# Five small moves in a two-layer decoder kernel: one output product dealt later in its turn, two copies shared between engines, two sets of tiles in other PSUM banks, and an earlier limit for the experts' statistics

## The chip, the cores and the metric

The kernel runs on one core of one Trainium2 chip. The metric is the device time in microseconds of one execution, lower is better. A core has a matrix engine (TensorE, PE in the profile; its weight loads are listed apart as PEld), a vector engine (VectorE, DVE), a scalar engine (ScalarE, ACT), GpSimd (POOL) and SyncE (SP), which here issues most of the DMAs. Each engine works through a queue of its own in order, and engines wait for one another by semaphores. TensorE writes its results to PSUM, eight banks of 128 partitions by 512 fp32 numbers, from which VectorE or ScalarE copy ("empty") them.

## The reference, cut to what matters

Two decoder layers over x (8 x 112 x 512), with a context of 8 x 375 x 128. All is fp32.

```python
x = x + attn0(layernorm(x))          # 32 heads of 64, 8 kv heads, rope, window 64, sinks
x = x + xattn0(layernorm(x), ctx)    # 16 heads; keys of the 375 context rows by low rank maps
x = x + ffn0(layernorm(x))           # ternary weights, gelu
x = x + attn1(layernorm(x))          # 16 heads of 128, 4 kv heads, rope, causal mask
x = x + xattn1(layernorm(x), ctx)    # 16 heads of 32, causal mask
x = x + ffn1(layernorm(x))           # two rounds of gated experts
```

In attention 0 and cross attention 0 a head's result is multiplied by its rows of an output matrix Wo and added to x. In cross attention 0, `ctx_lat = ctx_c @ w_kc_kv` and then `ctx_lat @ Wo.T`; both matrices are weights, so the kernel multiplies them with each other first ("folds" them) and uses the product.

## The kernel before, in words

**Tiles.** The 896 rows of x (8 batches of 112) stand in SBUF as 7 tiles of 128 rows, numbered 0 to 6. Transposed activations (xT) are in two halves of four batches, 448 columns each. A tile of x may straddle two batches, so it is complete for an output product only when certain batches are done (`completed`: after the first half of a turn pair tile 0 at once and tiles 1, 2 later; after the second half tiles 3, 4 at once and 5, 6 later).

**PSUM.** One pool with two buffers for each of three tags: `mm` (one bank, helper `mm`), `s` (two banks, helper `wide`, the score banks) and `t` (one bank, helper `turning`, for transposes). The third request for a tag waits until the first buffer has been emptied.

**Order of work.** TensorE's order is the order in which the program is written (its manual schedule). The other engines' orders are laid out by a planner, which simulates the program with costs of its own: of the instructions ready at a time it takes the one written first. `with tc.issue_after(i)` puts an instruction behind instruction i in the queue of its engine, if they are on the same one. `weave(main, filler)` (L237) deals filler steps between main steps: each step has a cost, and after a main step filler is taken as long as the cost of the filler done, plus half of the next one's, is at most the filler's total times the share of main done. The rest comes at the end.

**The attention pipeline (L410 to L457).** Attention 0 has 8 turns: 4 groups of 8 heads by 2 halves of the batches. Each turn has 4 units (a batch each). A unit's main steps are two transposes of the normalised probabilities p (ppt, L404, emptied to pT at L405), the scores two units ahead (ps, L608), and the contexts (po, L625, emptied to oT at L630). Softmax of a unit (L374 to L394): VectorE adds the mask (L382) and takes the maximum (L385), ScalarE does eight exponentials (L388), VectorE takes the reciprocals (L391), GpSimd scales (L393). A turn is two weaves: units 0 and 1, filled with the preparation of the next turn and then the late output products of the turn before; units 2 and 3, filled with the early output product of this turn. The lines are

```python
filler, late = ready or (prepare(n + 1) if n < end else []), outputs(n - 1, True) if n else []
ready, early = None, []
...
weave(mains(n, range(units - ahead)), filler + late)
...
weave(mains(n, range(units - ahead, units)), outputs(n, False) + early + extra(n))
```

Preparing a turn is one key and four query products (pr_k, pr_q: L235 called from L543), each followed by the rope: ScalarE copies with a bias (raw, L547), SP issues four DMAs that turn halves of the rows (L552), VectorE multiplies (L555), GpSimd multiplies and adds (L554, L556) into kT or qT. An output product (po_at, L361 and L365) is 4 matmuls with wo in two parts, and VectorE's addition to x (L366). Turn 7, the last, is woven in the next stage's `finale` (L878 for cross attention 0), with context transposes (pkv, L875), layernorm steps and the first fold.

**Cross attention 0.** A fold for each of 4 groups of 4 heads (`fold_steps`, L688 to L721): pB, four pV (L716, emptied to vo at L717) and two pR (L708, emptied to wr at L712), all in `mm` banks; the order is pB, pV, pV, pR, pR, pV, pV. Folds 1 to 3 are filler of the turns before their group (at about 433, 534 and 635 us). A turn's preparation: two query products pq_x (L235, emptied at L779) and eight key products pk_x (L783, emptied to kr at L784), a batch and half a group each. Odd batches use a `turning` bank, even ones an `mm` bank. Turn 0's keys stand in a list written by hand in `after` (L895), among transposes of x (pt_xa, L310).

**Cross attention 1, `go` (L1213).** There are sixteen units of softmax over 8 heads; the first five are woven together, with this filler: values pev (L1170, emptied to ev at L1171, odd batches of the second half by ScalarE, others by VectorE), the transposes of tiles 4, 5 and 6 (pt_xa, L310, in `mm` banks, emptied to xT by ScalarE at L314) and four query products peq. The later ones are woven one by one, with half an output product each (po_e, L361 and L365).

**The experts.** `ffn_1` begins with the layernorm of all 7 tiles into res (L1311; statistics L285, L286, root L274, scaling L289), each behind `copied[0]`, the last copy of transposed probabilities (L405). Then TensorE transposes res (pt_ff, L310) and does the first expert's products (pf).

Of the kernel before, what the change touches and what calls it, by code (L numbers as in the profile page):

```python
# [155 lines left out]
def decoder(ctx: ExitStack, tc: tile.TileContext, i: dict, out: bass.AP):  # L156
    nc = tc.nc
# [30 lines left out]
    x = cpool.tile([P, NT, D], F32, name="x")  # L188
# [4 lines left out]
    spans, n = _spans(_COLS)  # L193
# [7 lines left out]
    rspans, n = _spans(_ROWS)  # L201
# [14 lines left out]
    eps5 = cpool.tile([P, 1], F32, name="eps5")  # L216
# [9 lines left out]
    def wide(name):  # L226

        return psum.tile([P, 2, D], F32, tag="s", name=name)
# [8 lines left out]
    def weave(main, filler):  # L237


        whole, extra = sum(m[0] for m in main), sum(f[0] for f in filler)  # L240
        at, k, done, parted = 0.0, 0, 0.0, True

        def fill():
            nonlocal k, done, parted
            done += filler[k][0]
            filler[k][1]()
            k += 1
            parted = True

        for cost, step, *gap in main:  # L250
            if gap and not parted and k < len(filler):
                fill()
            step()
            parted = False
            at += cost
            while k < len(filler) and done + filler[k][0] / 2 <= extra * at / whole:
                fill()
        while k < len(filler):
            fill()

    def run(steps):
        for _, step, *_ in steps:
            step()
# [71 lines left out]
    def entering(pool, xT, name, tiles, bufs, bank=None):  # L335

        xn = {}

        def norm():
            xn.update(zip(tiles, normed(pool, tiles, name, bufs)))  # L340

        return [(0.0, norm)] + [(0.45, lambda k=k: turned_tile(xn[k], xT, k, name, bank)) for k in tiles]

    spread, copied = [], []


# [63 lines left out]
    def pipeline(turns, units, ahead, prepare, scores, contexts, outputs, extra, begun=None, finale=None, between=False, keys_early=()):  # L410

        queue = [(n, u) for n in range(len(turns)) for u in range(units)]

        def scored(k):
            return [(1.2, lambda: scores(*queue[k]))] if k < len(queue) else []

        def mains(n, us):
            steps = []
            for u in us:
                coming, own = scored(n * units + u + ahead), contexts(n, u)
                if between:
                    steps += own[:2] + coming + own[2:]
                else:
                    steps += coming + own
            return steps

        if begun is None:
            run(prepare(0) + extra(-1))
            for k in range(ahead):
                run(scored(k))
        for k in range(begun or (ahead if begun is None else 0), ahead):
            run(scored(k))
        end = len(turns) - 1
        ready = None
        for n in range(end + (finale is None)):
            filler, late = ready or (prepare(n + 1) if n < end else []), outputs(n - 1, True) if n else []  # L440
            ready, early = None, []
            if begun is None and n == 0:
                run(filler[:3])
                filler = filler[3:]
            weave(mains(n, range(units - ahead)), filler + late)
            if n in keys_early:
                early, *ready = prepare(n + 2)
                early = [early]
            weave(mains(n, range(units - ahead, units)), outputs(n, False) + early + extra(n))
        if finale is None:  # L450
            run(outputs(end, True))
        else:
            fillers, after = finale(outputs(end - 1, True) + outputs(end, False) + outputs(end, True))
            for u, filler in enumerate(fillers):
                weave(mains(end, [u]), filler)
            after()
# [231 lines left out]
    def fold_steps(pool, g, loads, kept):  # L688

        wq, woT, kk, ranks = loads  # L690
        rk = pool.tile([P, 4, 64], F32, tag="rk", bufs=1, name=f"rk_{g}")
        wr = pool.tile([P, NC, 256], F32, tag="wr", name=f"wr_{g}")
        vo = wpool.tile([P, 4, D], F32, tag="w", name=f"vo_{g}")
        kept.update(wr=wr, krw=ranks[:, 12:, :].rearrange("p a b -> p (a b)"), vo=vo)

        def rank():
            ps = mm(f"pB_{g}")
            for h in range(4):
                accumulate(
                    ps[:, h * 64 : (h + 1) * 64], [(kk[:, 3 * h + c, :], ranks[:, 3 * h + c, :]) for c in range(3)]  # L700
                )
            nc.vector.tensor_copy(rk.rearrange("p a b -> p (a b)"), ps[:, :256])

        def queries(c):
            ps = mm(f"pR_{g}_{c}")
            for k in range(2):
                for h in range(4):
                    nc.tensor.matmul(  # L708
                        ps[:, k * 256 + h * 64 : k * 256 + (h + 1) * 64],
                        wq[:, h, (c + k) * P : (c + k + 1) * P], rk[:, h, :], start=True, stop=True,  # L710
                    )
            nc.scalar.copy(wr[:, c : c + 2, :].rearrange("p a b -> p (a b)"), ps)  # L712

        def values(h):
            ps = mm(f"pV_{g}_{h}")
            nc.tensor.matmul(ps, kk[:, 12 + h, :], woT[:, h, :], start=True, stop=True)  # L716
            nc.vector.tensor_copy(vo[:, h, :], ps)  # L717

        v = [(0.9, lambda h=h: values(h)) for h in range(4)]
        q = [(1.7, lambda c=c: queries(c)) for c in (0, 2)]  # L720
        return [(2.5, rank), v[0], v[1], *q, v[2], v[3]]  # L721
# [27 lines left out]
    def cross_attention_0():  # L749
# [16 lines left out]
        def prepare(n):  # L766

            g, hf = turns[n]
            f, nm, qpool = folds[g], name(n), pool if hf else epool
            held[n].update(  # L770
                qr=[qpool.tile([P, HT], F32, tag="qr", name=f"qr_{nm}_{j}") for j in range(2)],
                kr=[qpool.tile([P, HB, L], F32, tag="kr", name=f"kr_{nm}_{j}") for j in range(2)],
            )

            def queries(j):
                ps = mm(f"pq_{nm}_{j}")
                at = slice(j * P, (j + 1) * P)
                accumulate(ps[:, :HT], [(f["wr"][:, c, at], xT[hf][:, c, :]) for c in range(NC)])
                nc.scalar.copy(held[n]["qr"][j], ps[:, :HT])  # L779

            def keys(j, b):
                ps = (turning if b % 2 else mm)(f"pk_{nm}_{j}_{b}")
                nc.tensor.matmul(ps[:, :L], f["krw"][:, j * P : (j + 1) * P], kvT[:, b, :], start=True, stop=True)  # L783
                nc.scalar.copy(held[n]["kr"][j][:, b % HB, :], ps[:, :L])  # L784

            steps = []
            for j in range(2):
                steps.append((3.0, lambda j=j: queries(j)))
                steps += [(0.65, lambda j=j, b=b: keys(j, b)) for b in batches(n)]
            return steps  # L790
# [354 lines left out]
    def cross_attention_1(npool, tpool):  # L1145
# [66 lines left out]

        def go():  # L1213
            values, queries, *outs = more
            enter = entering(npool, xT, "xa1", [4, 5, 6], 3, mm)
            fill = outs + enter[:1] + values[:2] + enter[1:2] + values[2:3] + enter[2:3] + values[3:]
            fill += enter[3:] + queries
            outs, units = outputs(), [divmod(k, 2 * HB) for k in range(4 * HB)]

            def steps(k):  # L1220
                *turn, add = contexts(*units[k])
                if k + 3 < len(units):
                    return turn + [(1.0, lambda: scores(*units[k + 3]), True), add[:2]]
                return turn + [add]

            scores(*units[2])
            weave([m for k in range(5) for m in steps(k)], fill)

            for k in range(5, len(units)):
                weave(steps(k), (outs[9:12] if k == len(units) - 1 else outs[k - 6 : k - 5]) if k > 5 else [])  # L1230
            run(outs[12:])
            pool.release()

# [52 lines left out]
    def ffn_1():  # L1286
        with (
# [3 lines left out]
            res = rpool.tile([P, NT, D], F32, tag="res", bufs=1, name="res")  # L1291
# [16 lines left out]
            w4 = rpool.tile([P, NT, P], F32, tag="w4", bufs=1, name="w4")  # L1308
            nc.gpsimd.memset(w4, 0.0)
            for tiles in GROUPS:  # L1310
                layernorm([x[:, k, :] for k in tiles], [res[:, k, :] for k in tiles], eps5, f"ff1_{tiles[0]}", copied[0])  # L1311
            for k in range(NT):
                with tc.issue_after(spread[0]):
                    nc.gpsimd.tensor_tensor(x[:, k, :], x[:, k, :], res[:, k, :], ALU.add)
# [115 lines left out]
            with tc.manual_schedule(engines={mybir.EngineType.PE}):  # L1430
                tail = []
                for j in range(2):
                    src, dst, base = (res, nxt, res) if j == 0 else (nxt, x, x)
                    xT, kept = new_halves(f"ff1_{j}"), {}
# [64 lines left out]
```

## Time and profile before

| | |
|---|---|
| median of 3 runs | 1862.39 us (1861.94 to 1867.62) |
| profiled execution, its own time | 1863.88 us |
| its span in the profile | 1862.0 us, 19727 instructions |
| mean granted TensorE clock | 0.996 |
| DMA | 108.68 MB, mean 58 GB/s |
| fp32 copy of 128x512 from PSUM | 0.69 us on VectorE (vo), 0.59 us on ScalarE (wr) |
| eight exponentials of a softmax | 3.0 us |

The profile's page gives, for one execution, each engine's busy time, the chain of work that ended last, and groups of instructions with their mean duration and the idle time before them. A line names the engine, the line of the kernel (it can be that of a helper: L235 is any accumulated product, L310 any transpose of activations), the output and its inputs. A wait "PE a <- ACT b" is time in which TensorE stood still before writing a, and the last thing it needed was ScalarE's b. The granted clock (PEclk) is the share of TensorE's full clock: 1.00 or, in a few stretches of 3.41 us, 0.50. Matmul ends are modelled, so a busy TensorE isn't always TensorE at full speed.

### The profile page before, as it was taken

The numbers are of one execution on the slowest core, as the hardware profiler recorded it, in microseconds if no ns is written. First come the engines' busy times: TensorE is split into PE (matmuls) and PEld (weight loads), VectorE is DVE, ScalarE is ACT, GpSimd is POOL, SyncE is SP. The second block draws the span as 40 slices with busy tenths as digits, with TensorE's granted clock in tenths as the row PEclk, the third lists the DMA queues.
The fourth block names the chain that finished last, engine by engine and source line by source line (L and its number), as shares of the span: only waits on it lengthen the run. The fifth ranks groups of instructions, "written<-read, shape, count | busy, mean of one in ns | idle before, by whom it ended". The sixth has DMA issues, their size and how long they took to land.

```text
span 1862.0 us, 19727 instructions
## 1 busy us (share of the span) xinstructions
PE 1814.6 (97%) x7088; PEld 982.4 (53%) x7088; DVE 791.2 (42%) x1389; ACT 656.6 (35%) x1946; POOL 586.3 (31%) x512
## 2 busy tenths in 40 slices
PE   8999999899999999989999999999999999999999
PEld 4454455545554555567655555545654444555444
DVE  5455666555454545767433233336721212221213
ACT  2444444454333334565222322346632121121120
POOL 3455544355555530000133343302321011011111
PEclk9999999999999999999999999999999999999999
DMA  6132323043242212011222131301020000000001
GB/s 236 26 120 79 127 86 122 27 138 109 50 136 53 49 40 91 23 68 68 61 69 71 30 85 30 138 1 46 4 107 1 1 0 0 0 0 1 0 0 40
DMA packets 35497, 108.68 MB, mean 58 GB/s; under 512 B 6644, under 2 KB 20012, under 8 KB 28744
## 3 DMA queue, kind: packets, MB, share of 16 engines
q1 hardware_dynamic: 28264, 77.97, 13.0%
q0 software_dynamic: 6848, 29.36, 5.4%
q8 instruction: 56, 0.92, 0.2%
q14 instruction: 41, 0.34, 0.1%
q10 hardware_dynamic: 288, 0.09, 0.0%
HBM read 78.83 MB, written 10.22 MB: 48 GB/s over the span
## 4 chain that ended last, share of the span: by engine, by line
PE 89%; DVE 5%; ACT 4%; POOL 1%; issue 1%; DMA 1%; SPq 0%; DVEq 0%; POOLq 0%; ACTq 0%
PE pf L235 16%; PE po L235 11%; PE pr_q L235 10%; PE po_at L361 5%; PE po_at L365 5%; PE po_x L838 4%; PE pv L235 3%; PE po L625 3%; PE ps L608 3%; PE pr_k L235 3%; PE po_x L361 3%; PE pq_x L235 2%; PE po_x L365 2%; PE ph L235 2%; PE ps_x L804 2%; PE po_ff L1078 2%
## 5 line engine op out<-in xcount | busy, mean ns | idle before, releaser
L235 PE MATMUL pr_q<-xT_at,wq 128*128 128x448 f32 x512 | 204.1, 543 | 0.0
L235 PE MATMUL pf<-xT_ff,fup 128*128 128x448 f32 x512 | 199.8, 541 | 1.6 <-ACT xT_ff L314 1.6
L1413 POOL TENSOR_TENSOR h<-silu,h 128x448 f32<-128x448 f32 x64 | 73.0, 1140 | 405.2 <-ACT silu L1412 405.1
L235 PE MATMUL po<-fdn,h 128*128 128x512 f32 x448 | 197.2, 592 | 0.0
L235 PEld LDWEIGHTS pf<-xT_ff,fup 128*128 128x128 f32 x512 | 96.0, 190 | 93.0 <-issue 87.2
L393 POOL TENSOR_TENSOR p<-p,total 112x896 f32<-112x896 f32 x48 | 83.3, 1737 | 181.0 <-DVE total L391 151.5
L1396 ACT ACTIVATE h<-pf,cols 128x448 f32<-128x448 f32 x64 | 40.6, 635 | 279.4 <-PE pf L235 276.9
L235 PEld LDWEIGHTS pr_q<-xT_at,wq 128*128 128x128 f32 x512 | 93.5, 190 | 84.6 <-issue 78.7
L235 PEld LDWEIGHTS po<-fdn,h 128*128 128x128 f32 x448 | 84.6, 190 | 100.6 <-issue 100.1
L388 ACT ACTIVATE p<-p,nmax 112x113 f32<-112x113 f32 x256 | 96.0, 379 | 109.4 <-DVE nmax L385 108.8
L361 PE MATMUL po_at<-wo,oT 128*128 128x512 f32 x224 | 109.4, 611 | 1.2 <-ACT oT L630 1.2
L365 PE MATMUL po_at<-wo,oT 128*128 128x512 f32 x224 | 105.3, 592 | 0.0
L235 PE MATMUL pf<-h,sw 128*128 128x448 f32 x256 | 101.5, 540 | 0.0
L556 POOL TENSOR_TENSOR qT<-qT,turned_q 128x448 f32<-128x448 f32 x64 | 75.2, 1178 | 55.1 <-DVE turned_q L555 48.6
L961 POOL TENSOR_SCALAR tl<-tr,ternary_bounds 128x512 f32<-128x512 f32 x32 | 52.0, 1625 | 125.8 <-DMA tr<-in_c_w_dram 125.8
L838 PE MATMUL po_x<-pT_x,kv 125*128 125x448 f32 x192 | 89.3, 549 | 1.2 <-DVE pT_x L833 0.8
L810 DVE TENSOR_REDUCE nmax_x<-ps_x 112x2 f32<-112x750 f32 x64 | 57.2, 934 | 76.4 <-PE ps_x L804 75.9
L554 POOL TENSOR_TENSOR qT<-raw_q,consts 128x448 f32<-128x448 f32 x64 | 78.5, 1231 | 25.2 <-ACT raw_q L545 19.0
L812 ACT ACTIVATE p_x<-ps_x,nmax_x 112x375 f32<-112x375 f32 x124 | 69.8, 575 | 43.9 <-DVE nmax_x L810 43.8
L1426 DVE SCALAR_TENSOR_TENSOR nxt<-po,wr,nxt 128x512 f32<-128x512 f32 x42 | 31.5, 751 | 120.6 <-PE po L235 120.6
L405 DVE COPY pT<-ppt 112x448 f32<-112x448 f32 x96 | 57.0, 616 | 59.5 <-PE ppt L404 59.5
L1426 DVE SCALAR_TENSOR_TENSOR x<-po,wr,x 128x512 f32<-128x512 f32 x42 | 31.5, 751 | 118.8 <-PE po L235 118.8
(252 smaller groups left out, 3199.9 us busy)
## 6 DMA issues: line engine op xcount, KB each, us to landing
tw<-in_c_w_dram SPq DMA_DIRECT2D x16, 512.0 KB
tr<-in_c_w_dram POOLq DMA_DIRECT2D x32, 256.0 KB, 4.3
signs<-tl POOLq DMA_DIRECT2D x32, 256.0 KB, 2.9
turned_q<-raw_q SPq DMA_DIRECT2D x128, 56.0 KB
turned_q<-raw_q SPq DMA_DIRECT2D x64, 112.0 KB
wq<-in_a_q_dram SPq DMA_DIRECT2D x4, 1024.0 KB
wo<-in_a_o_dram SPq DMA_DIRECT2D x4, 1024.0 KB
bq<-in_b_q_dram SPq DMA_DIRECT2D x4, 1024.0 KB
```

Source lines behind the costliest of these rows:

```text
L235: nc.tensor.matmul(ps, lhsT, rhs, start=(k == 0), stop=(k == len(pairs) - 1))
L361: nc.tensor.matmul(ps[0], lhsT, rhs, start=(c == 0), stop=False)
L365: nc.tensor.matmul(ps[0], lhsT, rhs, start=False, stop=(c == len(pairs) - 1))
L388: nc.scalar.activation(p[:, h, :], src[:, h, :], AF.Exp, bias=nmax[:, h : h + 1], accum_out=total[:, h : h + 1])
L393: spread[:] = [nc.gpsimd.tensor_tensor(p[:, :, :T], p[:, :, :T], total, ALU.mult).ins]
L554: nc.gpsimd.tensor_tensor(by_batch(dst), by_batch(raw), cos, ALU.mult)
L556: nc.gpsimd.tensor_tensor(dst, dst, turned, ALU.add)
L810: nc.vector.tensor_reduce(nmax, ps[:T, :, :L], AX.X, ALU.max, negate=True)
L812: e = nc.scalar.activation(p[:, 2 * j + s, :], ps[:T, s, :L], AF.Exp, bias=nmax[:, s : s + 1], accum_out=total[:, 2 * j + s : 2 * j + s + 1],)
L838: nc.tensor.matmul(po[0][:, : 4 * T], kv[:, b, c, :], pTs[c], start=(c == 0), stop=(c == NLC - 1))
L1413: nc.gpsimd.tensor_tensor(at["h3"][:, c, tokens], s, at["h1"][:, c, tokens], ALU.mult)
L1426: nc.vector.scalar_tensor_tensor(d, po, kept["w"][:, k, m - 2 : m - 1], d, ALU.mult, ALU.add)
```

## The change

- In turn 6 of attention 0 (`n == 6 and begun is None`: only attention 0 has `begun` None), the last of the late output products of turn 5, that of tile 6, is taken out of the first weave and put into the second, behind the early product of turn 6 and ahead of the four context ropes.
- The vo copies of odd heads go from VectorE to ScalarE.
- The key products of turn 0 of cross attention 0 all use `mm` banks.
- The transposes of tiles 4, 5 and 6 in cross attention 1 use the first half of a score bank pair.
- The experts' statistics stand behind the copy of transposed probabilities of the last unit but one, and no longer behind that of the last.

```diff
+    stats_behind = []
     spread, copied = [], []
...
             ready, early = None, []
+            if n == 6 and begun is None:
+                late, early = late[:-1], late[-1:]
...
-            nc.vector.tensor_copy(vo[:, h, :], ps)
+            (nc.scalar.copy if h % 2 else nc.vector.tensor_copy)(vo[:, h, :], ps)
...
-                ps = (turning if b % 2 else mm)(f"pk_{nm}_{j}_{b}")
+                ps = (turning if b % 2 and n else mm)(f"pk_{nm}_{j}_{b}")
...
-            enter = entering(npool, xT, "xa1", [4, 5, 6], 3, mm)
+            enter = entering(npool, xT, "xa1", [4, 5, 6], 3, lambda name: wide(name)[:, 0, :])
...
                 weave(steps(k), (outs[9:12] if k == len(units) - 1 else outs[k - 6 : k - 5]) if k > 5 else [])
+                if k == len(units) - 2:
+                    stats_behind[:] = copied
...
-                layernorm([x[:, k, :] for k in tiles], [res[:, k, :] for k in tiles], eps5, f"ff1_{tiles[0]}", copied[0])
+                layernorm([x[:, k, :] for k in tiles], [res[:, k, :] for k in tiles], eps5, f"ff1_{tiles[0]}", stats_behind[0])
```

## The prediction, made before the result was known

> **What bounds the kernel now.** I read the page first.
>
> ```profile
> PE 1814.6 (97%) x7088; PEld 982.4 (53%) x7088; DVE 791.2 (42%) x1389; ACT 656.6 (35%) x1946; POOL 586.3 (31%) x512
> ...
> PE 89%; DVE 5%; ACT 4%; POOL 1%; issue 1%; DMA 1%; SPq 0%; DVEq 0%; POOLq 0%; ACTq 0%
> ```
>
> TensorE has work in 1814.6 of 1862.0 us, and the chain that ended last runs over it for 89%. The change adds and removes no matmul, so all it can win is in the other 47 us and in what slows a matmul. Next, what TensorE waited for (total us, times, longest):
>
> ```profile
> PE ps L608 <- POOL qT L556: 2.1, 2, 1.6
> PE ppt L404 <- POOL p L393: 1.8, 1, 1.8
> ...
> PE pev L1170 <- ACT ev L1171: 1.7, 1, 1.7
> PE pt_ff L310 <- DVE res L289: 1.6, 2, 1.2
> ...
> PE pR L708 <- DVE vo L717: 1.6, 2, 1.3
> ...
> PE pt_xa L310 <- ACT kr_x L784: 0.9, 1, 0.9
> ```
>
> The last five are the five places of the change: 7.6 us together. Third, busy time by stretch, cut on the grid on which the granted clock changes (columns: us, then busy us of PE, PEld, DVE, ACT, POOL, then clock):
>
> ```profile
> core 0: us, PE busy (x) PEld busy (x) DVE busy (x) ACT busy (x) POOL busy (x), PEclk, DMA share, GB/s
> 326.94:330.36 3.42, 1.46 (x10) 0.99 (x10) 3.42 (x6) 0.61 (x2) 1.13 (x1) 1.00 0.00 0
> 330.36:333.77 3.41, 3.02 (x7) 1.83 (x8) 2.93 (x9) 3.33 (x17) 0.88 (x1) 0.50 0.00 0
> 1265.61:1269.02 3.41, 1.63 (x20) 1.28 (x20) 3.41 (x8) 3.40 (x18) 0.00 (x0) 1.00 0.00 0
> 1269.02:1272.44 3.42, 3.18 (x10) 1.69 (x12) 1.61 (x2) 3.07 (x15) 1.68 (x1) 0.50 0.04 7
> 640.97:644.38 3.41, 2.15 (x14) 1.40 (x12) 2.15 (x3) 0.00 (x0) 2.42 (x3) 1.00 0.19 70
> ```
>
> A stretch in which TensorE worked 1.46 or 1.63 us of 3.41 is followed by one at half clock; after 2.15 us it is not. Two more sites agree (1.37 and 1.72 us: halved; 2.00 us at 791: not). So some 1.7 us of idleness inside one grid window costs more than itself: at 330 four transposes and four matmuls took 3.6 us for 2.1 at full clock (1.5 lost), at 1269 values, transposes and contexts took 3.9 for 2.2 (1.7 lost).
>
> **A rule that speaks against this.** The Trainium skill, page "TensorE: Matmul & The Clock Gate", section "HAM oscillation — how this bites in real kernels", asks only for no idle gap over about 3.4 us. By it both stalls cost themselves alone (1.85 and 1.7); by the rows 3.3 and 3.4. I take the rows, and charge the same 1.7 for each new stall over 1.7 us.
>
> **1. The output product moved (turn 6 of the first attention).** Moving its 3.4 planner units changes the whole mix of the first half of the turn, since filler is dealt out by its share. Filler steps follow once their running cost, with half of the next, is below the main steps' share done; worked through with 22.7 units of filler (before) and 19.3 (after), the order before, which the trace shows, is: ... query product 2, second transposes, query product 3, scores, product of tile 5, contexts, product of tile 6 | transposes, first scores of turn 7. After: ... query 2, scores, query 3, contexts, product of tile 5 | transposes, first scores of turn 7, product of tile 0, contexts, transposes, product of tile 6. The moved product does come to lie in front of the 1.85 us wait on p (328.12). But it leaves its place between query product 3 and the first scores of turn 7, which need that query roped. From the end of query product 3 to those scores there were 9.9 us (308.06 to 317.96); there will be contexts 0.9 + product 3.6 + transposes 0.8 = 5.3.
> How long does the rope take? When scores go straight ahead of a query product, ScalarE runs that softmax's eight exponentials first. In turn 5 (time, duration, instruction):
>
> ```profile
> 252.61 1.04 PE L608 MATMUL ps<-kT,qT 64*112 64x112 f32 x16
> 253.58 3.27 PE L235 MATMUL pr_q<-xT_at,wq 128*128 128x448 f32 x8
> ```
> ```profile
> 256.42 0.39 ACT L388 ACTIVATE p<-p,nmax 112x113 f32<-112x113 f32 x1 [3.02 <-DVE nmax L385]
> ...
> 259.41 0.62 ACT L547 ACTIVATE raw_q<-pr_q,cols 128x448 f32<-128x448 f32 x1
> ```
>
> The product was done at 256.8; its copy came at 259.41, behind the exponentials. It is so in all five such places (55, 94, 174, 253, 293): 7.1 to 8.2 us from the scores' start to the copy's end. From there to the finished operand the two keys with an idle queue took 6.0 (172.38 to 178.34, 250.62 to 256.60: four SP issues of 0.6, landing, VectorE 0.6, GpSimd 1.1).
> After the change scores start at 305.05, so the copy ends at 312.2 to 313.2 and the query is ready at 318.2 to 319.2. TensorE reaches the scores at 314.5, does their first twelve matmuls (0.7), and stops about 3.5 us before the last four. (Even with the 9.9 us lead, turn 6's first scores waited 1.6 us on qT at 275.96: the 2.1 us of the first row above.) They end near 319.0 (before: 318.93). Then product 3.63 + contexts 0.90 + transposes 0.39 + moved product 3.63 + 0.39 + scores 0.97 + contexts 0.90 = 10.8: the last turn starts at 329.8 instead of 328.12: +1.7 (1.0 to 2.4). Its own p is ready by 328 (9.2 us after the scores before), so that wait is gone. Clock: 3.5 us idle halve a window (+1.7), the window at 330 is spared (-1.5). Sum **+1.9**. The four weight loads queued on SP behind the rope's DMAs start 3 us later; their first use is at 350. Below: if the copy goes ahead of the exponentials, query 3 is ready at about 316 and the edit gives -3.3+1.4 = -1.9 or, with no stall at all, -3.3.
>
> **2. Folded values (L717).** vo of odd heads goes to ScalarE: 8 copies, VectorE 0.69 each, on ScalarE 0.59 by the same shape (wr, L712). At 643.18 the product pR waited for the second vo, which stood on VectorE behind p_x (2.01 us). ScalarE is free from 640.92 to 645.21; the second pV ends at 641.2, so its copy ends at 641.85, and contexts keep TensorE busy to 641.92. Gain 1.26, and 0.32 at 440.45; the folds at 355 and 540 show no such wait. Nothing queues behind the copies (ScalarE's next work there waits on TensorE); at 356 it follows exponentials and oT. **-1.6** (-1.2 to -1.6).
>
> **3. Keys of turn 0 in mm banks (L782).** The wait of 0.86 at 394.37 is for a transposes' bank that a key copy frees. But the transposes also need xn of tile 6, done at 394.00: at most 0.3 to win. Against it: six key products now share two banks. The second must await the x addition (389.88, +0.3), the fifth the copy of the third, which stands behind ScalarE's table load and square root (391.6 to 393.2): it starts at 393.7, then two keys, and the transposes start at 394.9. **+0.6** (-0.3 to +0.7; with a halved window +2.2).
>
> **4. Transposes of tiles 4 to 6 in score banks.** pev of the third batch no longer waits 1.73 for ev. Next late is the chain to the first query product, which needs xT of tile 6: ScalarE does ev, xT (to 1269.7), then eight exponentials 3.07 from 1270.04, then xT, eoT, ev, xT, 0.55 each: done 1275.2. Before it started at 1275.91: -0.7. TensorE would idle from 1273.2 to 1275.2, 2 us: with chance a half it halves a window (+0.9); the loss at 1269 was mostly covered by the same ScalarE chain. A tile waiting in a score bank holds scores up only until its xT copy. Ends: -3.4 (copies ahead of the exponentials, both costs gone) and +1.0. I take **-0.4**, near the chain.
>
> **5. Expert statistics.** VectorE had nothing from 1341.5 but began there with the statistics; the transposes waited 0.41 + 1.25 for res and 0.24 for xT. Tiles 0 to 3 are summed by 1334.1, so four statistics (0.64 each), the root with its 1.28 table load and four scalings (0.54 to 0.95) fit between 1336 and 1346, ahead of 1348.49. Tile 4 follows by 1349.2. Then the transposes are paced by xT copies on ScalarE (0.59): the first expert product starts at 1351.6 for 1353.3. **-1.7** (-0.5 to -2.0). Exponentials end at 1335.3, so no table load is added.
>
> **Sum:** +1.9 -1.6 +0.6 -0.4 -1.7 = -1.2 us. The profiled execution took 1863.88 (span 1862.0), the median of three is 1862.39, inside their spread; on it: 1861.2.
>
> **Rivals.**
> A. Query 3's copy goes early: for it, at 308.1 with no exponentials ready it went at once; against it, five of five. Edit 1 gives -3.3: sum -6.4, 1856.0.
> B. Slower: half clock after new stalls. GpSimd's rope steps took up to 2.4[...], so the query may come at 320.5: the last turn +3.4, idle 5.3 us, two windows 3.2, spared 1.5: +5.1. With halved windows in 3 (+2.2) and 4 (+1.0): +5.0 in all, 1867.4. It decides where a grid window keeps under about 1.7 us of work.
> C. In 4 the copies go ahead of the exponentials: -3.0 more, 1858.2.
> D. The statistics are allowed sooner but planned no sooner (only the limit moves, the order is the planner's): without 5, 1862.9.
>
> **Numbers.** Forecast 0.45, A 0.15, B 0.13, C 0.15, D 0.12. 0.3% (5.6 us) is about what a measurement here can tell from no change: under 1856.8 or over 1868.0. Faster: most of A, a third of C, a little of the rest: 0.17. Slower: under half of B and unforeseen reorderings by the planner: 0.11. Range 1855.5 to 1867.5.
>
> **What would show it.** 1: TensorE waiting 3 to 4 us on qT (L556) near 315, no wait on p near 328, half clock after 317. 2: no wait on vo. 3: a wait of pk_x on kr_x near 393. 4: no wait on ev, instead peq on xT near 1275. 5: no wait on res, pf from 1351.6. Wrong if the rope copy precedes the exponentials, or if another engine's replanned order opens a wait elsewhere.

## The result and the profile after

The changed kernel takes 1868.34 us (median of 22 runs, 1866.72 to 1870.66), beside 1864.04 us for the kernel before in the same comparison (22 runs, 1861.54 to 1872.40): ratio 1.0021, 95% interval 1.0014 to 1.0029, so 4.3 us slower by the medians and 3.9 us (2.6 to 5.4) by the ratio. The forecast was 1.2 us faster. The 1862.39 us that the forecast stood on lies 1.65 us below the median of those 22 runs; the other 4.3 us are the change's. The profiled execution has a span of 1866.2 us (before 1862.0). From its page:

```profile
PE 1815.3 (97%) x7088; PEld 982.0 (53%) x7088; DVE 788.8 (42%) x1381; ACT 661.2 (35%) x1954; POOL 586.0 (31%) x512
```

TensorE is busy only 0.7 us longer (before 1814.6), so most of the 4.2 us of span is idleness of TensorE. The eight vo copies have gone from VectorE to ScalarE, as meant. What TensorE waited for (total us, times, longest):

```profile
PE ps L611 <- POOL qT L559: 6.6, 2, 5.0
...
PE peq L235 <- ACT xT_xa L314: 3.4, 2, 2.9
...
PE pk_x L786 <- ACT kr_x L787: 1.3, 1, 1.3
```

The waits on p, ev, res and vo that the change aimed at are gone from this list. Three others stand in their place: 5.0 us on qT, 2.9 on xT, 1.3 on kr_x. The largest is near 316 us. Around it, by stretches of the clock's grid (us, busy us of PE, PEld, DVE, ACT, POOL, then the granted clock):

```profile
315.95:319.36 3.41, 0.27 (x6) 0.09 (x2) 0.73 (x3) 0.00 (x0) 2.23 (x3) 1.00 0.45 91
319.36:322.78 3.42, 1.54 (x5) 0.95 (x6) 1.34 (x2) 0.00 (x0) 1.13 (x1) 0.50 0.89 355
322.78:326.19 3.41, 3.41 (x5) 1.35 (x4) 1.41 (x2) 1.87 (x10) 0.00 (x0) 0.50 1.02 432
```

TensorE worked 0.27 us in one window and 1.54 in the next, and two windows in a row were granted at half clock, 6.83 us together. The profile before had one hereabouts, at 330.36. And this is the way to the late query (start, duration, instruction):

```profile
305.90 1.04 PE L611 MATMUL ps<-kT,qT 64*112 64x112 f32 x16
...
309.01 1.08 DVE L383 TENSOR_TENSOR p<-ps,consts 112x896 f32<-112x896 f32 x1
...
314.67 0.62 ACT L550 ACTIVATE raw_q<-pr_q,cols 128x448 f32<-128x448 f32 x1
...
320.06 1.13 POOL L559 TENSOR_TENSOR qT<-qT,turned_q 128x448 f32<-128x448 f32 x1 [1.88 <-DVE turned_q L558]
...
321.24 0.72 PE L611 MATMUL ps<-kT,qT 64*112 64x112 f32 x4 [5.02 <-POOL qT L559]
```

The scores end at 306.94, but VectorE adds the mask only at 309.01. The eight exponentials follow, then query 3's raw copy at 314.67, the rope, and the scores that need it at 321.24.

To place gains and losses I matched matmuls of the two traces and followed by how much those of the changed kernel lag: +0.9 us by 290, where the program is still the same; then +5.2 to 365 (the product); +1.4 to 432 (the keys, and a wait of 0.7 on pT_x that comes and goes from trace to trace); -0.4 at 440 and -2.3 to 660 (values); -1.4 to 845 (before met half-clock windows at 808 and 818, this execution only one, at 814); +1.1 at 1255 to 1300 (the cross transposes); -0.4 at 1335 to 1375 (statistics). In sum +4.2 us.

### The profile page after: what moved, and what is told of

It reads as the page before. It is cut to its first block, busy times and chain, and to the rows that moved or that the text cites. A ratio compares the mean times of both kernels' runs of the same rounds, so it can differ in the third digit from the quotient of the medians.

```text
span 1866.2 us, 19719 instructions
## 1 busy us (share of the span) xinstructions
PE 1815.3 (97%) x7088; PEld 982.0 (53%) x7088; DVE 788.8 (42%) x1381; ACT 661.2 (35%) x1954; POOL 586.0 (31%) x512
## 4 chain that ended last, share of the span: by engine, by line
PE 87%; DVE 6%; ACT 3%; SPq 1%; DMA 1%; issue 1%; POOL 0%; DVEq 0%; POOLq 0%; ACTq 0%
PE pf L235 16%; PE po L235 10%; PE pr_q L235 9%; PE po_at L362 5%; PE po_at L366 4%; PE po_x L841 4%; PE pv L235 3%; PE pq_x L235 3%; PE pr_k L235 3%; PE po L628 3%; PE ps L611 3%; PE po_x L362 2%; PE ph L235 2%; PE po_x L366 2%; PE po_ff L1081 2%; PE ps_x L807 2%
## 5 line engine op out<-in xcount | busy, mean ns | idle before, releaser
L559 POOL TENSOR_TENSOR qT<-qT,turned_q 128x448 f32<-128x448 f32 x64 | 74.7, 1168 | 59.3 <-DVE turned_q L558 53.7
```

The lines of the kernel that those rows point to most:

```text
L559: nc.gpsimd.tensor_tensor(dst, dst, turned, ALU.add)
```

## The experiments

Theory: the product's move costs about 5 us by query 3's late copy, the cross transposes cost 1 us by the last tile's late copy, and the rest is a small gain. Rivals: the loss comes only of the parts together; or the move needs its 1.9 us of cover, however the steps are dealt; or the clock, and not the wait, is the price. Each ratio is against runs of the kernel before made in the same comparison (their medians lie between 1863.11 and 1864.39 us), and a gain or loss given for a run's time is worked out from its ratio.

**The product moved alone**

```diff
+            if n == 6 and begun is None:
+                late, early = late[:-1], late[-1:]
```

> Only the output product of turn 6 is moved; all else is as before. Theory (size): the matmuls of the changed kernel fell 4.9 us behind between 281 and 342 us, and the move alone does that: about 1868.5 to 1869 us, ratio 1.0026, with a stall of about 5 us on qT L559 near 315 and two half-clock windows behind it. Rival (interaction): the move alone costs the 1.9 us that was predicted, a stall of about 3.5 us and one half-clock window, and the rest came with another part of the change: about 1866 us, ratio 1.0010.

1869.7 us, ratio 1.0029 (1.0020 to 1.0038), a stall of 4.97 us on qT and two half-clock windows. The move alone costs what the whole change costs, within the intervals; the rival of an interaction falls.

**All but the product** (the change's diff without those two lines)

> The whole change without the product move. Theory: the rest of the change is worth -2.7 (values by two engines) +1.05 (keys) +1.1 (cross transposes) -0.4 (statistics) = about -1 us, and one half-clock window more or less by where the clock's grid falls (1.3 us): about 1863 us, ratio 0.9988 to 1.0000. Rival (the losses are not the move's): still about 1867 to 1868, ratio above 1.0015.

1864.91 us, ratio 1.0001 (0.9993 to 1.0009): the loss is gone, but the other four parts bring no gain that can be measured. They are taken apart below. In this trace the cross transposes cost 2.7 us, with two half-clock windows at 1275.

**The product moved, an empty step in its place**

```diff
+                late, early = late[:-1] + [(late[-1][0], lambda: None)], late[-1:]
```

> The product is moved, but a step of the same planned cost that does nothing stays in its old place among the steps of the first weave, so that every other step is dealt to the place that it had before. Theory (the moved product changes where the other steps are dealt, and so puts the raw copy of query 3 behind the exponentials): the copy of query 3 goes ahead of the exponentials, qT is late by 1 us or less, no wait on p, no half-clock window behind it: -1.5 to -2 us against before, 1862 us, ratio 0.9991. Rival (what is missing is the product's 1.9 us of cover ahead of the scores): still a stall of over 3 us on qT and a half-clock window: 1866 us or more, ratio 1.001 or more.

1863.09 us, ratio 0.9997 (0.9989 to 1.0005). The stall is 0.6 us. The timeline shows why: scores now follow the query product, so its copy is ahead of the exponentials, the first of which starts at 313.44.

```profile
308.90 1.04 PE L610 MATMUL ps<-kT,qT 64*112 64x112 f32 x16
309.06 0.63 ACT L549 ACTIVATE raw_q<-pr_q,cols 128x448 f32<-128x448 f32 x1 [2.78 <-PE pr_q L235]
...
313.44 0.39 ACT L388 ACTIVATE p<-p,nmax 112x113 f32<-112x113 f32 x1 [3.75 <-DVE nmax L385]
```

So the loss is that of the dealing order: with 3.4 units of filler fewer, `weave` put the scores ahead of the last query product. Of the missing cover only that stall of 0.6 us is left. But the expected gain isn't shown by the time, and the next comparison says where the trace's 1.3 us come from.

**What a half-clock window costs in this stretch.** Four lines, with the columns of the windows above, compare the stretch from turn 7's key product to the first fold's pR in four kernels. First before, one halved window:

```profile
290.57:365.07 74.50, 68.47 (x335) 36.58 (x333) 51.89 (x94) 32.55 (x123) 29.61 (x25) 0.98 0.20 69
```

Then a kernel of a later experiment (the transposes' copy by VectorE) with the same code here, which met two, 6.83 us from 330.07:

```profile
290.80:366.84 76.04, 70.02 (x334) 37.10 (x333) 52.70 (x94) 32.48 (x123) 31.26 (x25) 0.96 0.20 68
```

Then the combination without the move, which differs here by two vo copies and met none:

```profile
289.70:362.75 73.05, 67.04 (x335) 35.79 (x333) 51.24 (x93) 32.89 (x124) 30.11 (x25) 1.00 0.20 70
```

TensorE's idleness is 6.0 us in all three; only the busy time differs, by 1.4 to 1.6 us for a window. Where the grid cuts the same stalls decides how many follow. Before's halved window at 330.36 had TensorE busy for 3.02 us, and full clock came back; the other kernel's first one, which began earlier in the same waits, had 2.86 us, and a second followed:

```profile
330.07:333.49 3.42, 2.86 (x9) 1.74 (x9) 3.42 (x9) 2.75 (x14) 0.64 (x1) 0.50 0.00 0
```

Last, the moved product with the empty step:

```profile
291.40:364.58 73.18, 67.67 (x334) 35.79 (x333) 51.47 (x94) 32.42 (x123) 32.06 (x24) 1.00 0.21 70
```

It gains 1.3 us on before, but no more than unmoved code gains by meeting no halved window (1.45). What the move itself is worth, with the order kept, is about nothing. The wait on p is gone and the last turn starts some 0.6 us sooner, but within that turn 0.8 us are lost again, behind the waits on kvT that are shown with the next run.

**The move, with the idle time filled** (beside the move's two lines)

```diff
+            if l0 and (n, u) == (7, 0):
+                warm = mm("warm_7")
+                for k in range(5):
+                    nc.tensor.matmul(warm, ident, rows[:, :D], start=(k == 0), stop=(k == 4))
```

> The product moved alone, and five matmuls that no output depends on (some 4.3 us of work, into a tile that nothing reads) put on TensorE right ahead of the scores that wait for qT. It adds work that the reference doesn't have; the outputs are unaffected. Clock theory (of the 5 us that the move costs, about 3 are the two half-clock windows behind the stall, 2 or less the stall itself): qT comes when it did, the idle time is filled, no half-clock window follows, and it takes about 3 us less than the move alone: 1866.5 to 1867 us, ratio 1.0013. Rival (it is the stall that costs, the clock only follows): the same time as the move alone or more, 1869.5 us, ratio 1.0028 or above.

1868.02 us, ratio 1.0022 (1.0012 to 1.0031); qT came as late as in the move alone (the scores that need it start 15.3 us after the scores before them in both), after 4.56 us of filling and 0.55 us of waiting. The stretch, in the move alone and then here:

```profile
291.69:370.71 79.02, 69.31 (x335) 36.63 (x333) 50.44 (x94) 32.49 (x123) 30.24 (x24) 0.96 0.19 65
...
292.20:369.42 77.22, 71.92 (x344) 37.63 (x343) 50.46 (x94) 32.35 (x123) 30.27 (x25) 1.00 0.20 67
```

No half clock, and 77.22 us for 79.02 in the move alone: the two windows cost 1.8 us, not 3. Part of a halved window lay in the stall itself and cost nothing: 3.1 us of the two in the move alone, 1.9 us in the change, which by an estimate (half of the difference) is 0.6 of the 0.7 us that the change loses more. The other 2.7 of the 4.5 us need no clock: the last turn starts 3.3 us later than before (the stall of 5.1 us, less the 1.85 us of waiting on p), 0.8 us are lost within it, and before's own halved window, 1.4, is not met. The 0.8 us come with longer waits of the context's transposes, first before and then here:

```profile
PE pkv L875 <- ACT kvT L876: 0.6, 1, 0.6
...
PE pkv L881 <- ACT kvT L882: 1.5, 2, 0.9
```

With their wait on pT (1.3 us before, 1.0 here) that is 0.6 us more, and it is so in all five traces with the moved product and the ropes in their place. Why ScalarE's copy comes later there was not followed up. Neither theory fits: in the traces the stall is the larger part. By the times the move with and without the filling can't be told apart.

**The move, with four context ropes later** (beside the move's two lines)

```diff
-                return [(0.6, rope) for _, rope in joined[0]["ropes"][4:]]
+                return joined[0]["ropes"][:4] + [(0.6, rope) for _, rope in joined[0]["ropes"][4:]]
...
-                for k, rope in enumerate(joined[0]["ropes"][:4]):
-                    steps.insert(len(steps) - 3 + k, rope)
+                pass
```

> The product moved alone, with the first four rope steps of the context (L745 to L748 on VectorE) taken out of the turn's first half and put ahead of the other rope steps in its second half. Theory (VectorE did these steps ahead of the mask add of the scores, so the eight exponentials and with them the raw copy of query 3 behind them came 2 us later than worked out): the exponentials begin about 2 us sooner, the wait on qT is about 3 us in place of 5.0, and one half-clock window follows in place of two: 2 to 3 us less than the move alone, 1867 us, ratio 1.0014. Rival (the mask add waits for other VectorE work, or the raw copy is behind something else): a stall of 5 us as before, 1869.5 us.

1874.98 us, ratio 1.0061 (1.0046 to 1.0076): much slower. The mechanism was right, the forecast wrong. The mask add and the copy came sooner:

```profile
306.43 1.04 PE L609 MATMUL ps<-kT,qT 64*112 64x112 f32 x16
...
307.58 1.09 DVE L382 TENSOR_TENSOR p<-ps,consts 112x896 f32<-112x896 f32 x1 [1.63 <-PE ps L609]
...
313.24 0.61 ACT L549 ACTIVATE raw_q<-pr_q,cols 128x448 f32<-128x448 f32 x1
```

From the scores' start to the copy's end it is 7.4 us, for 9.3 with the rope steps in front. But the longest of TensorE's waits are now

```profile
PE ps L609 <- POOL qT L558: 3.0, 1, 3.0
PE pkv L876 <- DVE kv L746: 2.3, 1, 2.3
```

The context's transposes wait for the ropes that were put off, and windows of half clock follow for 10.24 us more at 336.

**The cross transposes alone, and with the last copy by VectorE**

```diff
-            enter = entering(npool, xT, "xa1", [4, 5, 6], 3, mm)
+            enter = entering(npool, xT, "xa1", [4, 5, 6], 3, lambda name: wide(name)[:, 0, :])
```

> Only the cross stage's last transposes moved into score banks. Theory (ScalarE's planned order puts the next unit's exponentials ahead of the last transposed tile's copy, so the product peq waits 2.9 us and the half-clock window falls behind that): a loss of 1.1 us as in the changed kernel to 2.7 us as in the run without the product move, by how many half-clock windows follow: 1865.5 to 1867 us, ratio 1.0006 to 1.0014. Rival (the score banks remove waits on free buffers and the loss is of another part): -0.7 us, ratio 0.9996.

1866.38 us, ratio 1.0013 (1.0006 to 1.0021). Tile 6's transposes are done at 1270.33, but eight exponentials stand ahead of its copy:

```profile
1269.73 0.60 PE L310 MATMUL pt_xa<-consts,xn_xa 128*128 128x128 f32 x4
1270.41 0.39 ACT L388 ACTIVATE p_e<-p_e,nmax_e 112x112 f32<-112x112 f32 x1
...
1273.39 0.56 ACT L314 COPY xT_xa<-pt_xa 128x512 f32<-128x512 f32 x1
1274.01 4.85 PE L235 MATMUL peq<-xT_xa,eq 128*128 128x448 f32 x8 [2.91 <-ACT xT_xa L314]
```

The product takes 4.85 us, because it falls into a halved window; with the copy by VectorE,

```diff
-            enter = entering(npool, xT, "xa1", [4, 5, 6], 3, lambda name: wide(name)[:, 0, :])
+            enter = entering(npool, xT, "xa1", [4, 5, 6], 3, lambda name: wide(name)[:, 0, :], nc.vector.tensor_copy)
```

(`entering` uses that last argument for the last tile's copy only)

> The transposes in score banks, with the last tile's copy made by VectorE in place of ScalarE. Theory: the copy no longer stands behind the exponentials, peq has no wait of 2.9 us and no half-clock window behind it: 2 to 4 us less than the transposes in score banks with ScalarE's copy, 1862.5 to 1863.5 us, ratio 0.9993. Rival (the copy waits for the transposes or for the bank, not for ScalarE): the wait stays above 2 us and the time is the same.

it is 1860.4 us, ratio 0.9985 (0.9977 to 0.9992), and peq takes 3.25 with no wait:

```profile
1270.99 0.60 PE L310 MATMUL pt_xa<-consts,xn_xa 128*128 128x128 f32 x4
...
1271.63 0.69 DVE L314 COPY xT_xa<-pt_xa 128x512 f32<-128x512 f32 x1 [1.46 <-PE pt_xa L310]
1272.46 3.25 PE L235 MATMUL peq<-xT_xa,eq 128*128 128x448 f32 x8
```

In the stretch from 1255 to 1300 the first kernel loses 1.2 us on before, the second gains 3.2, and the same 3.2 in the two combinations below. With the score banks in both, it is shown that ScalarE's queue holds the tile. VectorE's copy with the `mm` banks of before was not run, so whether the other banks are needed at all stays open.

**Values and statistics; keys alone; the statistics behind the reciprocal**

The values' and the statistics' lines of the change's diff alone:

> Only the two parts that the trace of the changed kernel shows with a gain: every second folded value emptied by ScalarE, and the statistics of the next stage planned sooner. Theory: -2.7 - 0.4 = about -3 us, 1861 us, ratio 0.9984. Rival (the gain of the values came out of other parts, such as the shifted clock grid): -1 or less, 1863 us, ratio 0.9995.

1862.04 us, ratio 0.9989 (0.9981 to 0.9998): -2.1 us, between the two that were named (-3.5 to -0.4 by the interval). The rest of my -2.7 for the values was not theirs: from 450 to 660 us the five traces with these copies gain 2.0 us on before and the eight without them 0.8, because before's profile has a wait of 0.8 us on pT_x at 555 that no other shows. With 0.4 at 440 the values give 2.0 - 0.8 + 0.4 = 1.6 us.

```diff
-                ps = (turning if b % 2 else mm)(f"pk_{nm}_{j}_{b}")
+                ps = (turning if b % 2 and n else mm)(f"pk_{nm}_{j}_{b}")
```

> Only the key products' tiles moved: in the first turn of the folded stage all four take mm tiles. Theory (four copies by one engine now stand between the products, so the third waits for a free tile): waits of 1 to 1.3 us in all on kr_x, a loss of about 1.0 us, 1865.4 us, ratio 1.0006. Rival (the wait moves from a later one and is not paid twice): no change within 0.4 us.

Ratio 1.0007 (0.9996 to 1.0017): the sign of so small an effect isn't settled by the time. The trace has the wait of pk_x on kr_x, 1.3 us as in the changed kernel, without the 0.9 on pt_xa that it replaces. From 365 to 432 us it loses 0.4 on before and 0.6 on the mean of the six other traces without the change and without a wait on pT_x there.

```diff
-                    stats_behind[:] = copied
+                    stats_behind[:] = inverted
```

(`inverted` holds the last reciprocal, L391 in the lines of before; the run has the change's lines on the statistics, with this one, and nothing else of it)

> Only the statistics of the expert stage planned sooner, but behind the last unit's reciprocal (L391) in place of the copy before it. Theory (in the changed kernel VectorE's first statistics stood ahead of that reciprocal and cost TensorE a wait of 0.80 us on p_e): that wait is gone, and the first product of the expert stage (pf) begins 1.0 to 1.7 us earlier than before: ratio 0.9992, 1862.7 us. Rival (what holds pf is the normalisation of x tiles that TensorE itself finishes late, and the stat's place doesn't matter): -0.4 us as in the changed kernel, ratio 0.9998.

Ratio 0.9999 (0.9991 to 1.0007): no gain in the time. In the trace the stretch from 1335 to 1375 gains 0.97 us, and 0.97 again in both combinations, against 0.38 in all three traces with the statistics as in the change. In the changed kernel VectorE took a statistic first:

```profile
1340.43 0.68 DVE L285 BATCH_NORM_STATS2 st_ff<-x 128x6 f32<-128x512 f32 x1
1341.03 0.19 DVE L392 RECIPROCAL total_e<-total_e 112x8 f32<-112x8 f32 x1
...
1343.12 0.60 PE L405 MATMUL ppt_e<-consts,p_e 112*112 112x112 f32 x4 [0.80 <-POOL p_e L394]
```

Behind the reciprocal the wait on p_e is back at the 0.20 of before:

```profile
1338.02 0.19 DVE L392 RECIPROCAL total_e<-total_e 112x8 f32<-112x8 f32 x1
1338.13 1.23 DVE L285 BATCH_NORM_STATS2 st_ff<-x 128x6 f32<-128x512 f32 x2
...
1340.12 0.60 PE L405 MATMUL ppt_e<-consts,p_e 112*112 112x112 f32 x4 [0.20 <-POOL p_e L394]
```

**The parts with a gain together.** Values by two engines, transposes in score banks with VectorE's copy, statistics behind the reciprocal; then the same with the moved product and the empty step. Their edits are the lines shown above.

> The parts with a gain together: values by two engines, the last cross tile's copy by VectorE with the transposes in score banks, statistics sooner behind the reciprocal; the product and the keys stay as before. Theory (the sections are far apart and add): -1.8 - 3.2 - 1 = -6 us, 1858 us, ratio 0.9968. Rival (the clock's grid gives part back: a half-clock window that one part takes away comes again elsewhere): -3.5 us, ratio 0.9981.

1857.95 us, ratio 0.9968 (0.9956 to 0.9980).

> The same, and the product moved with an empty step kept in its old place. Theory: -1.5 more than without the move, -7 us, 1857 us, ratio 0.9961. Rival (the move's gain of 1.3 us is a window that would have fallen elsewhere): the same as without the move.

1856.91 us, ratio 0.9961 (0.9949 to 0.9974). By the ratios the two combinations gain 6.0 and 7.3 us on before, and so beat the changed kernel too. The three parts give 1.6, 3.2 and 1.0 us alone by their traces: they add, as far as these runs can tell. Whether the moved product adds anything is not told; the intervals overlap almost wholly, and in the traces the stretch of the move takes 73.5 us with it and 73.0 without, no halved window in either.

## Why the prediction was wrong, point by point

| step | forecast | in the traces |
|---|---|---|
| 1 product | +1.9 | +4.5 alone, +5.2 in the change |
| 2 values | -1.6 | -1.6 |
| 3 keys | +0.6 | +0.6 |
| 4 cross transposes | -0.4 | +1.1 and +1.2 with one halved window, +2.7 with two |
| 5 statistics | -1.7 | -0.4 |
| sum | -1.2 | +4.2 to +4.9 with one halved window in 4; by the times +3.9 (2.6 to 5.4) |

**Step 1 failed in two terms.** The order dealt, the exponentials ahead of the copy, the wait on p gone and the 6.0 us from copy to finished operand (5.9) were as worked out. "7.1 to 8.2 us from the scores' start to the copy's end" was not: it took 9.4. The row came from five places in earlier turns, at which VectorE began the mask 1.1 us after the scores' start; in turn 6 it began 3.1 us after it, for VectorE had context ropes to do (L745 to L748 in the lines of after), which were written earlier and therefore planned first. So "about 3.5 us" of stall became 5.0. With the ropes out of the way it was 7.4 us and a stall of 3.0, inside the forecast. The last turn, forecast to start 1.7 us later, started 3.3 us later where the filling had taken the clock's part away.

The second term was put at nothing: what the last turn itself would lose. It was 0.8 us, behind the context's transposes. The clock's part was the smaller error: I charged one window at 1.7 and credited one at 1.5. There were two, which cost 1.8 together, and the credited one (1.4) was real but not the move's to give: it depends on where the grid lies. In sum 3.3 + 0.8 + 1.8 - 1.4 = 4.5, for 1.7 + 0 + 1.7 - 1.5 = 1.9.

Rival B, to which I gave 0.13, had the place, the late start of the last turn (+3.4), the idle time (5.3 us, measured 5.0) and the two windows. Its +5.1 for this step is close to what came, in part by luck: it had the windows 1.4 too dear and nothing for the 0.8, and its cause, a GpSimd step of 2.4 us, is not in the trace, where that step takes 1.13.

**Step 4** had its chain nearly right: peq was to start 0.7 us sooner and, with the lag taken off, started 0.3 sooner in the change and in the run alone. What failed is the "chance a half" of a halved window: TensorE was idle for 2.9 us, not 2.0, and all three traces show one or two. Of the ends named, the upper one (+1.0) held. The lower one was to be had (rival C's -3.4, measured -3.2), but by giving the copy to the other engine.

**Step 5** failed on the cover. The statistics did start as early as forecast, but they were not planned into VectorE's idle time only: the first went ahead of the last reciprocal, 0.6 us more of wait on p_e. The scalings did come 3.9 us sooner, and the waits on res (1.66) went; the transposes of the next tiles then waited 0.24 and 0.80 us on xT copies (0.24 before), one of which stood behind a root in ScalarE's queue. With the reciprocal mended it is -1.0; those copies are the other 0.7 of the forecast.

**Steps 2 and 3** held in the traces; by the times neither is settled alone. In 3 no window was halved.

**The rule weighed.** The Trainium skill's "TensorE: Matmul & The Clock Gate" ("HAM oscillation — how this bites in real kernels") asks for gaps over about 3.4 us. The gap of 5.0 us agrees with it; the window of before at 330 and the one behind 2.9 us of waiting in step 4 do not, and the code that meets no, one or two halved windows with the same 6.0 us of idleness shows that the grid's position decides there. The rows were the better guide to whether a window follows; they were too dear for one behind a long stall, and left out that a second may follow the first.

## What to carry to other kernels

When a step is taken out of a list that is dealt out by shares, every other step of the list may change its place: write the new order down, and ask for each engine what it now does first; an empty step of the same cost tests whether it is the step or the dealing. A delay taken from other places of the trace holds only where the same queues are empty: here 7.1 to 8.2 us became 9.4 by two microseconds of vector work that was written earlier. If a copy is ready and stands behind exponentials in one engine's queue, try the other engine too, and not only more buffers: here the buffers alone lost 1.1 to 2.7 us in the traces, and with VectorE's copy the same place gained 3.2.

## What the runs showed of the hardware

A half-clock window isn't the kernel's alone. The same code with the same 6.0 us of idleness met none, one or two in one stretch, and took 73.0, 74.5 to 74.7 or 75.6 to 76.0 us (two vo copies differ in some of them). A single trace is thus uncertain by about 1.5 us for each place of that kind; effects of this size need many runs or a stretch compared over several traces. A halved window that overlaps a long stall costs less: two of them 1.8 us, against 1.4 to 1.7 for one behind short stalls (the 1.7 at 1352 in the run of the cross transposes alone, in code that it leaves as before).

A halved window needs a busier TensorE to be followed by full clock than a full one does. Over the fourteen traces, of 41 windows at full clock in which TensorE was busy 1.73 us or less of 3.41, 38 were followed by half clock, and of those in which it was busy 1.85 us or more none was. But of nine halved windows with up to 2.87 us busy eight were followed by another, and of those with 3.02 us or more none was. At half clock a matmul takes twice as long (two of pev 2.05 us for 1.04 in the kernel before), so by an estimate the two limits lie near each other in work done. The ends of matmuls are modelled, and no run varies this alone.

What makes the wait of 0.7 to 1.1 us on pT_x near 420 appear in five traces of fourteen was not looked into.
